# Scoring layer 1's heads once instead of twice in a two-layer cross-attention kernel, with the banks and stops around it rearranged

## The chip, the cores and the metric

The kernel runs on one core of one Trainium2 chip, as one launch. A core has five engines that run their own queues in order and wait for one another through semaphores: TensorE (PE: matrix products and transposes into the accumulators, PSUM), VectorE (DVE), ScalarE (ACT), GpSimd (POOL) and SyncE (SP, which here issues nearly all DMAs). PSUM has eight banks of 128 x 512 floats. The metric is the device time of the launch in microseconds, as the median of several runs. All data are 32-bit floats.

## The reference

Two cross-attention layers, one after the other, each with a residual. The batch is B = 4, queries S = 512, width C = 320, 20 heads of 16; the context has T = 1024 rows of E = 512.

```python
# layer 0: text = rows 0..1019 of the context, ip = its last 4 rows
q = heads(x @ W_q); k = heads(text @ W_k); v = heads(text @ W_v)
probs = softmax(q k^T / 4);  text_out = probs v
qsem  = l2norm(probs @ text_rows)            # every head times the whole context: the heavy product
fused = q k_ip^T / 4 + 0.5 * (qsem . l2norm(ip_rows))
ip_out = (softmax(fused) * mask) v_ip
x = (text_out + ip_out) @ W_out + b_out + x
# layer 1: text = rows 0..76, ip = rows 77..1023, each with its own softmax
q = heads(x @ Wq^T)
out = softmax(q k^T / 4) v  +  softmax(q k_ip^T / 4) v_ip
x = out @ Wo^T + bo + x
```

Layer 1 of a query tile needs layer 0 of the same tile, and nothing of other tiles.

## The kernel before

**Tiles.** Queries go in 16 tiles of 128 (`TURNS`, four per batch entry). The 20 heads go in groups of four, so that there are 80 groups of layer 0 (`G`). A group is two units (`Unit`) of two heads. A unit multiplies the exponentiated scores with the context by a scheme with seven block products in place of eight: each `product` is four fp32 products of 128 x 128 by 256 or 277 columns (the profile counts each as two matmuls, so x8). The seven lie in four parts: `part0` does "11" and "12"x"21", `part1` does "t1" and "s2"x"t2", `part2` does "12"x"22" and "21"x"t3", `part3` does "t4". The later ones add onto the banks of the earlier ones: "t4" is added onto the bank of "11" after DVE has read it in `part2` (`add_square(self.b1, ...)`, the second instruction named `c`).

**Scores of layer 0.** The next group's scores are made transposed (keys on partitions) by `fill`, in two halves. A head has only 16 channels, so four heads lie in four groups of 32 rows of the PE and are computed beside each other; such a stretch of matmuls is called a visit to the row groups here. ACT copies the scores to SBUF and DVE takes maxima of them. `max0` transposes the four heads' maxima (4 transposes), DVE reduces them and transposes the small result (`zt`), and since the maxima are needed along the free dimension of every partition they take a way through DRAM: four DMAs write `zd`, one DMA reads it back into all partitions (`bc`). `do_exp` then adds the negated maximum to the scores on DVE (`e<-e,bc`), and ACT exponentiates. The four additions of a group wait in the queue `ew`.

**Scores of layer 1.** They are computed twice. `do_max` computes them with the queries on partitions (name `mx`, 512 columns at a time), DVE reduces them to maxima; `do_sub` transposes these (`pt_nm`) and adds them as extra channels to the queries (`qa`); `do_exp` computes the scores again, transposed and with the maximum already subtracted (name `ex`), so that ACT can exponentiate straight from PSUM. `step(g, k)` does one quarter of a group: `mx` of the next group in two of the row groups and `ex` of this one in the other two. `do_pv` multiplies with the values (72 small matmuls); `normalise` divides by the sums.

**Order.** All is written out by hand: PE and DVE instructions are kept in program order, ACT, POOL and SP are ordered by a scheduler that respects dependences. After each part of a unit comes a stop, so a group has stops 0 to 7 (`stop(gi, k)`). Before, a stop takes one waiting item (a piece of layer 0's end, `late`, or of the next batch entry's projections, `proj`), then `fill0` at stops 0 and 1, a layer 1 quarter at stops 2, 4, 5 and 6, `max0` at stop 2, and additions from `ew` at stops 4 (one), 5 (two) and 6 (one). That makes six visits to the row groups per group. SP has among its DMAs the windows (`window`): after each of the products "11", "21", "t1" and "t4" a small DMA brings the next unit's value columns, and must wait on SP until PE has done with the old ones.

**PSUM.** Two double banks for scores (`ps_sc`), three banks for products (`qs0` to `qs2`, the unit's b1, b2, b3 in turn), one for everything else (`tp`).

## Time and profile before

| What | Value |
|---|---|
| Time, median of 3 runs (lowest, highest) | 3527.53 us (3527.39, 3540.56) |
| Profiled execution | 3535.14 us, of which the span is 3533.4 us |
| Mean granted TensorE clock | 0.981 of full speed |
| Busy: PE, DVE, ACT, POOL | 98%, 58%, 42%, 28% of the span |
| First product of a unit, end of the last one | 92.3 us and 3393.4 us into the span |
| DMA | 252.5 MB, 71 GB/s |

Busy time of an engine is the time in which at least one of its instructions is open. On PE, matmuls in different row groups and successive matmuls overlap, so the busy times of two groups of matmuls that run side by side must not be added. How long a stretch really holds the PE is read in the timeline, from the start of its first matmul to the start of what follows.

### The profile page before, as it was taken

Reading aid. Unit: us, or ns where it says so; the run is one execution under the profiler, and the core shown is the slowest. Engines: PE = TensorE matmul, PEld = TensorE weight load, DVE = VectorE, ACT = ScalarE, POOL = GpSimd, SP = SyncE. Lnnn points to the kernel's source line nnn. Section 1 sums busy time; section 2 is a strip of 40 time slices with the busy share of each in tenths; the row PEclk is TensorE's granted clock in tenths of the full one; section 3 lists DMA queues with packets and bytes.
Section 4 is the critical chain, followed back from the end, with each engine's and each line's share of the span. In section 5 each row is a group of like instructions: output and inputs, shape, how many; then the busy total and the mean of one; then the engine's idle time right before and its main releaser. Section 6 shows DMA issues by size and latency. Waiting matters only on the chain.

```text
span 3533.4 us, 74393 instructions
## 1 busy us (share of the span) xinstructions
PE 3446.9 (98%) x29092; PEld 2770.0 (78%) x29092; DVE 2066.4 (58%) x3894; ACT 1477.4 (42%) x2807; POOL 1004.2 (28%) x1066
## 2 busy tenths in 40 slices
PE   7999999999999999999999999999999999999989
PEld 6777777777788888887878888877877878788766
DVE  2444556666655655566665665666665666666644
ACT  1333344444434444444443443444444444454422
POOL 3322222332222222333222222222322322332310
PEclk9999999999999999999999999999999999999976
DMA  7454332222344234222234434222232222222211
GB/s 213 105 134 116 89 70 41 47 39 48 88 98 102 62 101 105 51 56 42 47 88 111 101 75 100 67 55 49 45 85 46 47 40 51 44 45 43 46 30 34
DMA packets 618013, 252.54 MB, mean 71 GB/s; under 512 B 484112, under 2 KB 591344, under 8 KB 617664
## 3 DMA queue, kind: packets, MB, share of 16 engines
q1 hardware_dynamic: 616624, 244.18, 29.8%
q8 instruction: 231, 3.78, 0.5%
q0 software_dynamic: 864, 3.41, 0.4%
q14 instruction: 118, 0.97, 0.1%
q10 hardware_dynamic: 176, 0.20, 0.0%
HBM read 206.63 MB, written 40.33 MB: 70 GB/s over the span
## 4 chain that ended last, share of the span: by engine, by line
PE 84%; DVE 8%; DMA 3%; issue 2%; SPq 2%; ACT 1%; POOL 0%; DVEq 0%; POOLq 0%; ACTq 0%
PE b L77 51%; PE ex L77 6%; PE pv L77 5%; PE sc L77 4%; PE pt_v L77 4%; PE mx L77 4%; PE pt_k L77 4%; DVE m L87 2%; PE pt_y L77 2%; PE pt_q L77 2%; DVE e L87 2%; DMA bc<-zd 1%; PE mx L92 1%; DVE den L87 1%; DVE n L87 1%
## 5 line engine op out<-in xcount | busy, mean ns | idle before, releaser
L77 PE MATMUL b<-xv_t,e 128*128 128x277 f32 x2560 | 678.6, 407 | 16.1 <-DVE c L87 14.7
L77 PE MATMUL b<-xv,e 128*128 128x277 f32 x2560 | 627.0, 397 | 2.8 <-ACT e L785 2.8
L77 PEld LDWEIGHTS b<-xv,e 128*128 128x128 f32 x2560 | 480.2, 190 | 119.3 <-ACT e L785 3.3
L77 PEld LDWEIGHTS b<-xv_t,e 128*128 128x128 f32 x2560 | 462.0, 190 | 139.1 <-DVE c L87 19.6
L785 ACT ACTIVATE e<-e 128x1024 f32<-128x1024 f32 x320 | 338.2, 1057 | 385.0 <-DVE e L87 373.4
L874 POOL TENSOR_TENSOR e<-e,s 128x512 f32<-128x512 f32 x160 | 203.3, 1271 | 1010.1 <-PE b L77 983.0
L87 DVE TENSOR_REDUCE m<-sc 128x256 f32<-128x1024 f32 (+1 forms) x320 | 341.7, 1088 | 163.7 <-PE sc L77 156.0
L87 DVE TENSOR_REDUCE m<-mx 128x2 f32<-128x870 f32 (+3 forms) x345 | 366.6, 1066 | 88.5 <-PE ex L77 67.4
L585 ACT ACTIVATE e<-ex 128x1024 f32<-128x1024 f32 x320 | 325.2, 1017 | 187.3 <-PE ex L77 186.8
L87 DVE TENSOR_TENSOR e<-e,bc 128x1024 f32<-128x1024 f32 x320 | 354.1, 1107 | 73.3 <-DMA bc<-zd 73.3
L524 ACT COPY e<-sc 128x1024 f32<-128x1024 f32 x320 | 322.6, 1011 | 173.8 <-PE sc L77 135.1
L859 ACT ACTIVATE junk<-c 128x256 f32<-128x256 f32 x480 | 198.9, 414 | 460.0 <-DVE c L87 455.4
L77 PE MATMUL mx<-kq,qq 16*128 16x512 f32 x1280 | 375.7, 662 | 6.5 <-DMA qq<-q1d 3.8
L77 PE MATMUL ex<-qa,kq 19*128 19x128 f32 x5120 | 377.4, 288 | 4.0 <-DVE qa L87 3.1
L87 DVE TENSOR_TENSOR c<-b,p 128x256 f32<-128x256 f32 x320 | 133.5, 417 | 407.7 <-PE b L77 399.9
L855 POOL TENSOR_TENSOR s<-e,e 128x512 f32<-128x512 f32 x160 | 203.5, 1272 | 468.9 <-ACT e L785 299.7
L77 PEld LDWEIGHTS ex<-qa,kq 19*128 19x128 f32 x5120 | 319.2, 191 | 16.4 <-issue 5.8
L77 PE MATMUL b<-xs,e 128*128 128x256 f32 x1280 | 321.5, 394 | 5.0 <-DVE sums L87 2.8
L787 POOL TENSOR_TENSOR e<-e 128x512 f32<-128x512 f32 x160 | 209.0, 1306 | 388.6 <-ACT e L785 388.4
L77 PE MATMUL b<-xs_t,e 128*128 128x256 f32 x1280 | 304.1, 381 | 0.0
L77 PE MATMUL b<-xs_t,s 128*128 128x256 f32 x1280 | 302.3, 379 | 0.0
L77 PEld LDWEIGHTS b<-xs_t,s 128*128 128x128 f32 x1280 | 242.4, 189 | 39.7 <-ACT p L873 0.5
(192 smaller groups left out, 4185.0 us busy)
## 6 DMA issues: line engine op xcount, KB each, us to landing
kq<-kd SPq DMA_DIRECT2D x640, 64.0 KB
v1q<-v1d SPq DMA_DIRECT2D x80, 373.5 KB
bc<-zd SPq DMA_DIRECT2D x80, 256.0 KB
xv<-v0d SPq DMA_DIRECT2D x320, 42.0 KB
xv_t<-v0d SPq DMA_DIRECT2D x320, 42.0 KB
L_xattn_W_k<-in_L_xattn_W_k_dram SPq DMA_DIRECT2D x13, 640.0 KB
L_xattn_Wv_ip<-in_L_xattn_Wv_ip_dram SPq DMA_DIRECT2D x13, 640.0 KB
raw<-in_ctx_dram SPq DMA_DIRECT2D x32, 256.0 KB
```

The source lines that it names most:

```text
L77: tc.keep_in_program_order(nc.tensor.matmul(out, lhsT=lhsT, rhs=rhs, start=start, stop=stop, skip_group_check=on))
L87: return lambda *args, **kw: keep(getattr(self.engine, name)(*args, **kw))
L92: tc.keep_in_program_order(nc.tensor.transpose(out, in_, ident))
L524: nc.scalar.copy(e[i].rearrange("p h t s -> p (h t s)"), ps[i].rearrange("p h n -> p (h n)"))
L585: nc.scalar.activation(e.rearrange("p i j s -> p (i j s)"), ps.rearrange("p i n -> p (i n)"), AF.Exp)
L785: nc.scalar.activation(flat, flat, AF.Exp)
L787: nc.gpsimd.tensor_tensor(e[:, 1], e[:, 1], e[:, 0], ALU.subtract)
L855: nc.gpsimd.tensor_tensor(self.s2, self.e("21"), self.e("22"), ALU.add)
L859: nc.scalar.activation(junk, x, AF.Square, accum_out=self.w["ss"][:, self.h + r, k : k + 1])
L874: nc.gpsimd.tensor_tensor(self.e("11"), self.e("11"), self.s2, ALU.add)
```

## The change

For all query tiles but the last, layer 1's scores are computed once, in the manner of layer 0 (class `Once`): `fill` makes them transposed in two halves, ACT copies them to SBUF, DVE takes maxima. `maxima` transposes eight tiles (the first key tile of each head, which holds the 77 text rows, and the maxima of the rest), DVE makes four small reductions or minima and one small transpose, four DMAs write the result to DRAM, and three DMAs read it back into all partitions: text maxima for partitions 0 to 76, the others' for 77 to 127 and for the other tiles. `do_exp` adds them on DVE (six additions per group in two shapes) and exponentiates from SBUF on ACT. `mx`, `ex`, `pt_nm` and `qa` are left only in the last tile (`twice`).

The stops are regrouped. Layer 0's `fill0` goes to stops 0 and 2, layer 1's `fill` to stops 4 and 6: four visits per group. The four odd stops take the additions: layer 1's two and two at stops 1 and 3, layer 0's two and two at stops 5 and 7. Projections and the items behind go to odd stops too. `maxima` of layer 1 comes between the two products of unit 0's `part0`, `max0` between those of unit 1's. The values of layer 1 (`add_values`) come at stop 4.

The general PSUM pool `tp` gets two banks, and the products only two: b2 and b3 of a unit now share one. There are four instead of six buffers for layer 1's scores.

```diff
-    e1p = pool("e1p", 6)
+    e1p = pool("e1p", 4)
-    ps_tp = pool("ps_tp", 1, space=PSUM)
+    ps_tp = pool("ps_tp", 2, space=PSUM)
...
-            self.bank = [f"qs{(2 * gi + i + k) % 3}" for k in range(3)]
+            self.bank = [f"qs{(i + k) % 2}" for k in (0, 1, 1)]
...
-        def part0(self):
+        def part0(self, between):
             self.product(self.b1, "11", "11", True)
...
+            between()
             self.product(self.b2, "12", "21", True)
...
+    def spread(zt, rows, tag, name):
+        zd = dr.tile([rows, P], F32, tag=tag, name=f"{tag}{name}")
+        for k in range(P // ZW):
+            nc.sync.dma_start(zd[:, ZW * k : ZW * (k + 1)], zt[ZW * k : ZW * k + rows, :])
+        return zd
...
+    class Once:
+        def fill(self, c):
...
+            self.e[c] = fill(1, self.k, c, self.m, e1p, "e1", self.name)
...
+        def maxima(self):
+            first, rest = [tp(f"mx{self.name}_{k}").rearrange("p (h t) -> p h t", h=4) for k in range(2)]
+            for h in range(4):
+                tr(first[:, h, :], self.e[0][h // 2][:, h % 2, 0, :], ident)
+            for h in range(4):
+                tr(rest[:, h, :], self.m[:, 0, h, :], ident)
+            z = zz[1]
+            vec.tensor_reduce(z[:, 0:4], first[:, :, 0:NTXT1], AX.X, ALU.max, negate=True)
+            vec.tensor_reduce(z[:, 8:12], first[:, :, NTXT1:], AX.X, ALU.max, negate=True)
+            vec.tensor_reduce(z[:, 4:8], rest, AX.X, ALU.max, negate=True)
+            vec.tensor_tensor(z[:, 4:8], z[:, 4:8], z[:, 8:12], ALU.min)
+            zt = st2.tile([P, ZW], F32, tag="zt", name=f"zt{self.name}")
+            vec.transpose(zt, z)
+            zd = spread(zt, 8, "zd1", self.name)
+            self.bc = bc = big.tile([P, 2, 4, P], F32, tag="bc1", name=f"bc{self.name}")
+            keep(nc.sync.dma_start(bc[:NTXT1, 0], zd[0:4, :].partition_broadcast(NTXT1)))
+            keep(nc.sync.dma_start(bc[NTXT1:, 0], zd[4:8, :].partition_broadcast(P - NTXT1)))
+            keep(nc.sync.dma_start(bc[:, 1], zd[4:8, :].partition_broadcast(P)))
+            self.v = load_values(self.z, self.turn, self.g)
+
+        def do_exp(self, c, i):
+            e, (first, rest) = self.e[c][i], [self.bc[:, k, 2 * i : 2 * i + 2, :] for k in range(2)]
+            if c == 0:
+                vec.tensor_tensor(e[:, :, 0, :], e[:, :, 0, :], first, ALU.add)
+            x = e[:, :, 1 - c :, :]
+            vec.tensor_tensor(x, x, rest.unsqueeze(2).to_broadcast([P, 2, TH - 1 + c, P]), ALU.add)
+            flat = e.rearrange("p h t s -> p (h t s)")
+            nc.scalar.activation(flat, flat, AF.Exp)
...
+    def visit(gi, k):
+        if k < 4:
+            fill0(gi + 1, k // 2)
+        if k == 4:
+            do_values()
+            begin()
+            do_fill(0)
+        if k == 6:
+            do_fill(1)
+
     def stop(gi, k):
-        behind = k == 0 and after
-        if not behind:
-            item()
-        if k < 2:
-            fill0(gi + 1, k)
-        if behind:
-            after.popleft()()
-        if k in (2, 4, 5) or k == 6 and gi < len(G) - 2 or ending[0] and k < 2:
-            l1_step()
-        if k == 2:
-            max0(gi + 1)
-        end_stop(k)
+        if k in (1, 3):
+            do_adds(2)
+        elif k % 2:
+            for _ in range(2):
+                item(ew)
+        if k % 2:
+            item(after, late)
+            item(proj)
+        else:
+            if k:
+                item(late)
+            visit(gi, k)
+        if k == 3:
+            item(norm)
+        stops[0] += 1
...
-            for k, part in enumerate((u.part0, u.part1, u.part2, u.part3)):
+            between = (lambda: max0(gi + 1)) if i else do_maxima
+            for k, part in enumerate((lambda: u.part0(between), u.part1, u.part2, u.part3)):
                 part()
                 stop(gi, 4 * i + k)
```

The order of the built instructions shows what the scheduler makes of it on SP: between the four DMAs that write layer 1's maxima and the three that read them back stands the window of "21" in most groups, and the window of "t1" in 39 of 75.

## The prediction

> **What bounds the kernel now.** I read the engines' busy shares first, then the PE timeline of a late group without projections, then DVE's waits, then DVE and SP around one round trip of the maxima.
>
> ```profile
> PE 3446.9 (98%) x29092; PEld 2770.0 (78%) x29092; DVE 2066.4 (58%) x3894; ACT 1477.4 (42%) x2807; POOL 1004.2 (28%) x1066
> ```
>
> PE is the bound; DVE has slack. By groups, `mx` is busy for 375.7 us and `ex` for 377.4 us, 9.4 us per group. That is not what they cost: they run in different row groups at once. The timeline of one group:
>
> ```profile
> 3287.49 1.17 PE L77 MATMUL sc<-qq,kq 16*128 16x128 f32 x32
> 3288.60 2.14 PE L77 MATMUL b<-xv_t,e 128*128 128x277 f32 x8
> ...
> 3297.15 0.70 PE L77 MATMUL mx<-kq,qq 16*128 16x512 f32 x2
> 3297.16 0.71 PE L77 MATMUL ex<-qa,kq 19*128 19x128 f32 x8
> 3297.68 0.59 PE L77 MATMUL mx<-kq,qq 16*128 16x512 f32 x2
> 3297.71 0.61 PE L77 MATMUL ex<-qa,kq 19*128 19x128 f32 x8
> 3298.25 0.66 PE L92 MATMUL mx<-ident,m 128*128 128x128 f32 x4
> 3298.75 2.04 PE L77 MATMUL b<-xv_t,e 128*128 128x277 f32 x8
> ...
> 3325.94 1.17 PE L77 MATMUL sc<-qq,kq 16*128 16x128 f32 x32
> ```
>
> From start to next start a visit costs 1.10 us, layer 0's (3287.49 to 3288.60) as a layer 1 quarter (3297.15 to 3298.25); four transposes cost 0.50. The period is 38.45 us, 35.76 without the output projection in it (2.69). All 80 groups, from 92.3 to 3393.4 us, average 41.3 with projections.
>
> ```profile
> DVE e L87 <- DMA bc<-zd: 73.3, 43, 4.6
> PE b L77 <- DVE c L87: 14.7, 17, 1.6
> ...
> 2994.84 0.21 DVE L87 STREAM_TRANSPOSE zt<-zz 128x32 f32<-128x32 f32 x1
> 2995.26 1.28 SPq L772 DMA_DIRECT2D zd<-zt  x4
> 2998.59 0.34 SPq L774 DMA_DIRECT2D bc<-zd  x1
> 3002.16 1.23 DVE L87 TENSOR_TENSOR e<-e,bc 128x1024 f32<-128x1024 f32 x1 [0.64 <-DMA bc<-zd]
> ```
>
> The first two lines are us in total, times, longest. The others are the price of a round trip through DRAM: 7.1 us from the end of `zt` to the first addition (0.2 until SP issues, 3.3 from the first write's issue to the read's, 3.6 to the data). Even now, with nearly two stops between `zt` and the first addition, DVE is late in 43 groups; PE rarely notices (14.7 us in all).
>
> **The change, part by part.**
>
> *PE.* Layer 1 costs 4 x 1.10 + 0.11 (`pt_nm`) = 4.51 us per group; after, 2 x 1.10 + 8 transposes at 0.12 = 3.15. It saves 1.36 in each of 75 groups (the last tile's five keep two scorings): **-102 us**. A plain group's PE work becomes 34.4.
>
> *DVE.* Gone per group: reductions 2 x (1.222 + 1.052 + 0.311), 2 x 0.218 and `qa` 0.29 = 5.9. New, by the nearest forms: reductions from the accumulators 2 x (0.957 + 1.220), maximum 0.69, three small reductions 0.47 + 0.36 + 0.68 (by columns, between 0.311 at 154 and 0.684 at 512), 0.2, `zt` 0.21, additions 2 x (0.40 + 0.988 + 1.226) = 12.2. So 6.3 x 75 = 475 us more, 2066 to about 2540: under PE, but a plain group's DVE work (these, layer 0's, `c`, `p`, `den`) sums to 31.1 of 34.4 us.
>
> *ACT, POOL, SP.* ACT gains four copies of 1.011 and 0.04 on each of four exponentials: 4.2 x 75, to about 1795 us. POOL's operations stay. SP issues seven more DMAs per group, 0.35 each, and about 512 KB more are read; `bc`'s three reads wait on SP behind the window of "21", in 39 of 75 groups behind that of "t1", and with them all later windows and loads.
>
> *The new wait.* DVE runs in order: the additions at stops 1 and 5 stand ahead of the two `c` of `part2`, and "t4" on PE waits for the second `c`. The maxima are now made only one part earlier. Plain group, us from the start of unit 0's "11":
>
> PE: "11" 1.9, eight transposes 2.9, "12"x"21" 4.8, visit 5.9, `part1` (3.80) 9.7, `part2` (3.65) 13.35, visit 14.45: ready for "t4".
> DVE: small reductions and `zt` 4.45; `c`, `pv`, reductions, `p` until 8.9; then idle. SP: write 4.5, reads from 7.8 (behind "t1"'s window 8.3) 0.35 apart, the last landing at 13.0 with 0.4 for twice the bytes. Additions until 15.3, two `c` 0.75: "t4" starts at 16.1, PE waits **1.7**.
> DVE goes on without a gap: reductions 1.9, 0.69, 0.96, `pv` 0.17, additions 2.45, `den` 2.19, `zz` and `zt` 0.9: 25.3. PE had its transposes at 20.5. "t1" of unit 1 writes the bank of `b2`, so it waits for `c` and `pv`: 25.85 against 25.6 (**0.25**, the cost of two banks). Maxima land at 25.3 + 7.1 = 32.4, additions 2.65, two `c`: 35.8; PE was ready at 34.4, waits **1.4**. The next "11" starts at 37.8, but DVE has reductions, maximum and additions (5.9) before layer 1's small reductions and comes to them 1.4 late, which returns at the next "t4" as 0.6 to 1. Period about **38.7**: DVE's 31.1 and two idle waits of some 4 us. The loop is DVE plus round trips, no more PE.
>
> *Groups without projections.* 45 steps for each of three batch entries and 13 at the start, four odd stops per group: 37 groups have projections, 43 none. The end of layer 0 and the output projection hold PE for 8.6 us per tile (the timeline's `pt_s` 0.3, `pt_p` 0.2, `pt_ip` 0.6, `pt_o` 0.4, `pt_y` 1.7, `pt_xT` 0.4, `pt_q` 2.2 and 2.7), DVE for some 9 by its rows: 1.6 to 1.7 of PE per group (five to a tile), and on DVE 1.8, of which I count 1.3, as the rest falls into its idle waits. After: 38.7 + 1.3 = 40.0, PE work 34.4 + 1.6 = 36.0, idle 4.0, against some 0.5 before: 43 x 3.5 = **+150 us**. Bounds: every wait hidden (-0.5 x 43 = -22), or both 2 us longer, as the longest wait for `bc` (4.6) against the average (1.7) shows to be possible (+320).
>
> *Groups with projections.* A step holds PE 1.0 to 3.6 us, and four of them cover the wait. Their evacuations (0.24 to 0.69) stand on DVE behind the additions: +1 in 32 groups with layer 1, **+32 us** (0 to +80).
>
> *Tail.* Before, 140 us lie behind the last product. After, one group of layer 1 and half another are left, and their waits for `bc` stand on DVE in front of layer 0's end: +8 to +16; with them finished early, the last tile runs alone from the queries' arrival (3429): -9. I take **+5** (-10 to +20). Six fewer to four buffers and the start cost nothing: the values at stop 4 free the scores before the next copy.
>
> Sum: -102 + 150 + 32 + 5 = +85 on the profiled execution's 3535.1: 3620. That execution stands 0.2% above the median, so **3612**.
>
> **Two rules against the rows.** A PE wait of 1.50 us in the tail, among sparse row-group matmuls, was followed by a lower clock:
>
> ```profile
> 3396.00:3398.60 2.60, 1.10 (x3) 0.29 (x2) 2.35 (x9) 0.89 (x2) 0.00 (x0) 1.00 0.10 25
> 3398.60:3402.40 3.80, 3.80 (x73) 3.35 (x72) 2.05 (x7) 0.00 (x0) 0.00 (x0) 0.56 0.02 4
> ```
>
> The last three columns are clock, DMA share and GB/s. Among dense products 1.25 us (3280.4 to 3281.7) did nothing: the mean clock from 3200 to 3350 is 1.00. My waits of 1.4 to 1.7 lie near both; I take no loss, and price the loss below. The Trainium skill (TensorE: Matmul & The Clock Gate, HAM oscillation) says that gaps above about 3.4 us lower the clock: by it the sum stays, since no wait here is so long; the tail's row speaks against it. The skill also gives about 2.0 us as fixed cost of a transfer (DMA: Bandwidth & Descriptors): two would make a round trip of some 4 us and the sum an estimated 3 us per round trip smaller, so faster than before; the row of 7.1 decides.
>
> **Rivals.**
> 1. *The waits are hidden; faster.* For it: PE's saving is sure, and before, DVE's 73 us of waiting cost PE 15. Against: the distance shrank to about 5 to 9 us of PE work. It decides where the 40.0 us fall below 38.0 (then 43 x 1.5 us of idle more than before, 32 and 5 use up the 102), that is with each round trip 1 us shorter than in my ledger. With no wait left at all: 3535 - 102 - 22 + 5 = 3416. With 36.8, little more idle than before: 3535 - 102 + 43 x 0.3 + 5 = 3451, by the median **3443**. Chance 0.20.
> 2. *About the same.* Half of the +150 and the rest as forecast: 3535 + 10, by the median **3537**. Chance 0.10.
> 3. *The clock falls after each wait.* One window of some 3.8 us at 0.56 loses 1.7 us, twice per plain group: 43 x 3.4 = 146 more, **3758**. Against it: dense products on both sides. Chance 0.07.
> 4. *Two banks cost.* If DVE is later still, "t1" waits for `c` and `pv` in both units, 1 us each in 75 groups: +150, **3762**. For it: the ledger gives DVE no gap before. Chance 0.05.
>
> **How the numbers follow.** The forecast has 0.58 and, by itself, 3560 to 3680. 0.5% (18 us) is about what a measurement can tell from no change. Faster by more: 0.20; within: 0.10; slower by more: 0.58 + 0.12 = 0.70. The range 3480 to 3720 leaves out some 0.10 below and 0.08 above.
>
> **What would show it.** Right: DVE's wait for `bc` grows from 73 to 400 us or more; PE's wait for `c` from 15 to some 200; PE busy falls to about 92%, DVE rises to about 70%; a plain group lasts 39 to 41 us with "t4" late twice. Wrong: a period near 36, or the read of `zd` landing before `p`. The weakest link is the round trip's length when SP has windows ahead of it.

## The result and the profile after

The changed kernel takes 4010.62 us (median of four, 4001.30 to 4016.56), beside 3533.48 us for the kernel before, measured in turn with it. The ratio is 1.1347, with a 95% interval from 1.1308 to 1.1386: 477 us slower. The forecast was 3612 us, with 3480 to 3720 as its range. The direction was right, the size was not.

From the page of the changed kernel: the span, the busy lines of PE and DVE, the granted clock in 40 slices, and the shares of the chain that ended last.

```profile
span 3999.4 us, 74611 instructions
...
PE 3484.2 (87%) x28417; PEld 2774.1 (69%) x28417; DVE 2656.5 (66%) x4413; ACT 1764.7 (44%) x3107; POOL 1063.3 (27%) x1066
...
PEclk9999999999999999999899999989999999999976
...
PE 47%; DVE 26%; DMA 12%; issue 6%; ACT 4%; SPq 3%; POOL 1%; DVEq 0%; POOLq 0%; ACTq 0%
```

PE is idle for 3999.4 - 3484.2 = 515 us, against 3533.4 - 3446.9 = 86 before: 429 us more. PE's busy time rose by 37 us as well, although a group's visits to the row groups went from six to four. Idle and busy together are the 466 us between the two spans. PE has 84% of the chain before, and 47% after.

The waits of PE (first five lines) and two of DVE's (last two lines) in the changed kernel: total us, times, longest.

```profile
PE b L77 <- DVE c L87: 132.6, 86, 4.5
PE b L77 <- DVE pv L87: 102.5, 38, 6.0
PE b L77 <- DMA zd<-zt: 33.9, 6, 6.7
PE mx L92 <- DVE zz L87: 33.6, 7, 4.9
PE mx L92 <- DVE xT L87: 29.8, 8, 4.6
...
DVE e L87 <- DMA bc<-zd: 497.3, 154, 7.0
...
DVE m L87 <- ACT e L519: 109.5, 144, 1.9
```

The first line is the wait that the forecast had: "t4" waits for the second `c`, which stands behind additions that wait for `bc`. The second is another one: "t1" waits for `c` and `pv` of `b2`, because `b2` lies in the bank that "t1" is to write. The third has the same place: it comes at the end of a tile, where the norms stand on DVE ahead of `c` and `pv`.

The name that the profile gives to a wait is that of the semaphore that moved last, and can be the wrong one. So the idle times in the brackets of PE's timeline were also added up by place in the group. "t1" of unit 0 is late by 150.5 us in all (41 times), "t1" of unit 1 by 23.5 (35 times), "t4" by 95.0 in unit 0 (47) and 37.6 in unit 1 (39), and the transposes ahead of "12"x"21" by 72.5 in unit 0 (17) and 24.1 in unit 1 (34). That is 403 of the 515 us. All 54 starts of "t1" that are over 0.3 us late come 0.2 to 0.35 us after the end of `pv`, whatever name the profile gives. The transposes of unit 0 (the fourth and fifth line are most of them) need a general bank: in 10 of the 17 places they start 0.06 us after DVE has copied a transposed input (`xT` or `cT`) out of one. These copies come behind the additions of stop 7. The last line is a wait of DVE itself: its second reduction of a visit reads the half of the scores that ACT copies first, and waits for that copy.

From the page's groups of the changed kernel, busy us and mean ns of one:

```profile
L77 PE MATMUL b<-xv_t,e 128*128 128x277 f32 x2560 | 785.0, 455 | 307.8 <-DVE c L87 132.6
```

Two groups of the changed kernel with different forms kept apart:

```profile
L87 DVE TENSOR_TENSOR e<-e,bc 128x1024 f32<-128x1024 f32 x310 | 431.4, 1412 | 195.2 <-DMA bc<-zd 195.2
...
L87 DVE TENSOR_TENSOR zz<-zz 128x4 f32<-128x4 f32 x75 | 42.5, 566 | 2.6
```

The same matmuls of "t1" and "t4" (the first group) were busy for 678.6 us before. The five groups of block products (tile `b`) together went from 678.6 + 627.0 + 321.5 + 304.1 + 302.3 = 2233.5 us to 785.0 + 684.8 + 326.4 + 304.6 + 302.4 = 2403.2 us, so by 170 us, for the same work; without them PE's busy time fell by 132 us. Additions of 1024 columns grew from 1226 to 1412 ns, and the minimum of four columns (`zz`) takes 566 ns on average.

One group without projections shows all of it. The timeline of PE, DVE, POOL and SP in the changed kernel (start, duration, engine, line; in brackets the idle time before it and its releaser); the group's "11" is the first line:

```profile
3532.59 2.03 PE L77 MATMUL b<-xv,e 128*128 128x277 f32 x8
...
3535.35 2.04 PE L77 MATMUL b<-xv,e 128*128 128x277 f32 x8
3537.32 1.17 PE L77 MATMUL sc<-qq,kq 16*128 16x128 f32 x32
3541.70 4.03 PE L77 MATMUL b<-xv_t,e 128*128 128x277 f32 x8 [3.21 <-DVE pv L87]
3545.52 2.95 PE L77 MATMUL b<-xs_t,s 128*128 128x256 f32 x8
...
3554.25 3.82 PE L77 MATMUL b<-xv_t,e 128*128 128x277 f32 x8 [1.22 <-DVE c L87]
```

```profile
3534.11 0.69 DVE L87 TENSOR_TENSOR m<-m 128x512 f32<-128x512 f32 x1
3534.72 0.17 DVE L87 TENSOR_TENSOR pv<-b,p 128x21 f32<-128x21 f32 x1
3534.81 3.19 DVE L87 TENSOR_TENSOR e<-e,bc 128x1024 f32<-128x1024 f32 x2
3537.92 0.47 DVE L87 SCALAR_TENSOR_TENSOR e<-e,drop,bc 128x256 f32<-128x256 f32 x1
3538.31 1.34 DVE L87 TENSOR_REDUCE zz<-mx 128x4 f32<-128x308 f32 x3
3539.69 1.11 DVE L87 TENSOR_TENSOR zz<-zz 128x4 f32<-128x4 f32 x1
3540.84 0.21 DVE L87 STREAM_TRANSPOSE zt<-zz 128x32 f32<-128x32 f32 x1
3540.97 0.38 DVE L87 TENSOR_TENSOR c<-b,p 128x256 f32<-128x256 f32 x1
3541.27 0.17 DVE L87 TENSOR_TENSOR pv<-b,p 128x21 f32<-128x21 f32 x1
...
3551.03 2.50 DVE L87 TENSOR_TENSOR e<-e,bc 128x256 f32<-128x256 f32 x4 [4.75 <-DMA bc<-zd]
```

```profile
3539.53 1.25 POOL L940 TENSOR_TENSOR e<-e,s 128x512 f32<-128x512 f32 x1
```

```profile
3541.08 1.30 SPq L531 DMA_DIRECT2D zd<-zt  x4
...
3545.76 0.38 SPq L886 DMA_DIRECT2D xv_t<-v0d  x1
3546.32 0.32 SPq L584 DMA_DIRECT2D bc<-zd  x1
```

DVE works from 3534.11 to 3541.44 without a gap: the maximum, the two additions of stop 7, the small reductions, `zt`, and only then `c` and `pv`. `b2` was done at 3537.4, and PE's visit at 3538.5. So "t1" starts at 3541.70, 3.21 us late. Then it takes 4.03 us in place of 2.1. Its window on SP (L886) waits for its end and stands ahead of the reads of `bc`, which go out at 3546.32; with the 3.3 us of before between the issues of the first write and of the first read it would be 3544.4. The additions wait 4.75 us for them, and "t4" is late by another 1.22 us and slow as well. `zt` ends 8.46 us after the start of "11"; the forecast's ledger had 4.45, or 5.85 with the 1.4 us of lateness that it names.

### The profile page after: what moved, and what is told of

Same layout as the page of the kernel before. It is cut to its first block, busy times and chain, and to the rows that moved or that the text cites. A ratio compares the mean times of both kernels' runs of the same rounds, so it can differ in the third digit from the quotient of the medians.

```text
span 3999.4 us, 74611 instructions
## 1 busy us (share of the span) xinstructions
PE 3484.2 (87%) x28417; PEld 2774.1 (69%) x28417; DVE 2656.5 (66%) x4413; ACT 1764.7 (44%) x3107; POOL 1063.3 (27%) x1066
## 3 DMA queue, kind: packets, MB, share of 16 engines
q8 instruction: 227, 3.72, 0.4%
## 4 chain that ended last, share of the span: by engine, by line
PE 47%; DVE 26%; DMA 12%; issue 6%; ACT 4%; SPq 3%; POOL 1%; DVEq 0%; POOLq 0%; ACTq 0%
PE b L77 28%; DVE e L87 12%; DMA bc<-zd 10%; DVE m L87 7%; PE sc L77 4%; PE pt_k L77 3%; PE pv L77 3%; DVE zz L87 3%; PE pt_v L77 3%; PE pt_q L77 2%; ACT e L519 1%; ACT junk L922 1%; DVE den L87 1%; PE mx L92 1%; DMA zd<-zt 1%
## 5 line engine op out<-in xcount | busy, mean ns | idle before, releaser
L87 DVE TENSOR_TENSOR e<-e,bc 128x768 f32<-128x768 f32 (+2 forms) x770 | 785.8, 1066 | 498.8 <-DMA bc<-zd 497.3
L77 PE MATMUL b<-xv_t,e 128*128 128x277 f32 x2560 | 785.0, 455 | 307.8 <-DVE c L87 132.6
L87 DVE TENSOR_REDUCE m<-sc 128x256 f32<-128x1024 f32 (+1 forms) x620 | 667.0, 1088 | 300.1 <-PE sc L77 186.1
L77 PE MATMUL b<-xv,e 128*128 128x277 f32 x2560 | 684.8, 412 | 2.8 <-ACT e L848 2.8
L519 ACT COPY e<-sc 128x1024 f32<-128x1024 f32 x620 | 610.4, 1007 | 103.9 <-PE sc L77 63.3
L937 POOL TENSOR_TENSOR e<-e,s 128x512 f32<-128x512 f32 x160 | 234.1, 1463 | 1297.1 <-PE b L77 1260.5
L596 ACT ACTIVATE e<-e 128x1024 f32<-128x1024 f32 x300 | 316.3, 1057 | 407.8 <-DVE e L87 394.7
L848 ACT ACTIVATE e<-e 128x1024 f32<-128x1024 f32 x320 | 337.7, 1057 | 340.2 <-DVE e L87 339.1
L77 PEld LDWEIGHTS sc<-qq,kq 16*128 16x128 f32 x9920 | 309.4, 188 | 106.6 <-issue 91.8
L77 PE MATMUL sc<-qq,kq 16*128 16x128 f32 x9920 | 369.1, 285 | 5.5 <-DVE m L87 3.3
L77 PE MATMUL b<-xs_t,s 128*128 128x256 f32 x1280 | 326.4, 401 | 0.0
L77 PE MATMUL b<-xs,e 128*128 128x256 f32 x1280 | 304.6, 381 | 0.0
L77 PE MATMUL b<-xs_t,e 128*128 128x256 f32 x1280 | 302.4, 379 | 0.0
L77 PEld LDWEIGHTS b<-xs_t,e 128*128 128x128 f32 x1280 | 243.2, 190 | 33.1
L77 PEld LDWEIGHTS b<-xs,e 128*128 128x128 f32 x1280 | 239.2, 190 | 36.3 <-issue 2.0
L940 POOL TENSOR_TENSOR e<-e,s 128x512 f32<-128x512 f32 x160 | 214.5, 1341 | 127.0 <-PE b L77 126.5
L77 PE MATMUL pv<-e,v1q 128*32 128x128 f32 x5760 | 195.2, 287 | 44.8 <-ACT e L596 27.4
```

The lines of the kernel that those rows point to most:

```text
L77: tc.keep_in_program_order(nc.tensor.matmul(out, lhsT=lhsT, rhs=rhs, start=start, stop=stop, skip_group_check=on))
L87: return lambda *args, **kw: keep(getattr(self.engine, name)(*args, **kw))
L519: nc.scalar.copy(e[i].rearrange("p h t s -> p (h t s)"), ps[i].rearrange("p h n -> p (h n)"))
L596: nc.scalar.activation(flat, flat, AF.Exp)
L848: nc.scalar.activation(flat, flat, AF.Exp)
L937: nc.gpsimd.tensor_tensor(self.e("11"), self.e("11"), self.s2, ALU.add)
```

## The experiments

Two theories at the start. A, the forecast's: the additions' wait for the maxima's round trip, ahead of the copies `c`, is the cost. B: the bank that "t1" shares is the larger one, through `c` and `pv` behind late DVE work and the clock after that wait. All edits are to the changed kernel unless another is named. The medians of the kernel before that stand beside the runs lie between 3530.9 and 3538.8 us, so the base moves by some 0.2% from run to run; executions of one version differ by up to 0.7% (e12).

**Three product banks (e1).**

```diff
-    ps_tp = pool("ps_tp", 2, space=PSUM)
+    ps_tp = pool("ps_tp", 1, space=PSUM)
...
-            self.bank = [f"qs{(i + k) % 2}" for k in (0, 1, 1)]
+            self.bank = [f"qs{(2 * gi + i + k) % 3}" for k in range(3)]
```

So that one general bank is enough, `maxima` now makes its first two reductions ahead of the second four transposes.

> Three product banks again, everything else as in the changed kernel (4010.6 us). Theory A, the forecast's: the additions' wait for the maxima's round trip, ahead of the copies c, is what the change costs. It would leave VectorE's wait for bc near 500 us and TensorE's wait for c near 130 us, and give 3960 to 4000 us. Theory B: the product bank that t1 shares is the larger cost, because t1 waits for copies that stand behind late VectorE work (102.5 us for pv), the clock falls after that wait (170 us more on the product rows), and the window of t1 holds the reads of bc back on SP. It would take the wait for pv to under 20 us, bring the product rows back from 2403 to about 2250 us, and give 3700 to 3800 us.

4284.76 us (ratio to before 1.2115, 1.2065 to 1.2166): both theories missed. PE's waits in it:

```profile
PE mx L92 <- DVE zz L87: 220.2, 75, 6.2
PE pv L77 <- DVE zz L87: 111.6, 38, 6.5
...
PE b L77 <- DVE c L87: 28.3, 18, 5.9
```

The wait of "t1" for `pv` is out of the list, and the one for `c` is down to 28.3 us. But now the one bank left for everything else is held by the first four transposes until DVE has reduced them, so the next four (`mx`), and layer 1's values (`pv`) behind layer 0's maxima, wait for the same late DVE. Eight banks aren't enough for both; the queue on DVE is the same, only which of PE's steps waits for it has changed. That speaks for the queue as the cause, and against the bank by itself.

**Additions behind both copies (e2).**

```diff
-        if k in (1, 3):
+        if k in (2, 3):
             do_adds(2)
-        elif k % 2:
+        elif k in (6, 7):
```

> The eight additions go to stops 2, 3, 6 and 7 in place of 1, 3, 5 and 7, so that none stands ahead of both copies c; banks as in the changed kernel. Theory A: TensorE's wait for c falls from 132.6 to under 40 us, VectorE's wait for bc from 497 to under 250 us, and the time to about 3750 us. Theory B: the wait of t1 for pv (102.5 us) and the low clock after it stay; the time falls by no more than 100 us, to 3900 us or more.

4133.25 us (1.1687, 1.1646 to 1.1728). DVE's wait for `bc` fell from 497 to 14.3 us, and the time rose by 123 us. What took its place on PE:

```profile
PE mx L92 <- DVE m L87: 184.2, 95, 2.6
PE b L77 <- DVE pv L87: 103.1, 47, 6.0
```

Two additions at stop 2 and two at stop 6 now stand ahead of a visit's reductions, the maximum and the transposes that need it. Theory A's 3750 fell. The wait for `pv` is untouched, as theory B had it.

**Additions that wait for nothing (e3).**

```diff
+    zc = cst.tile([P, 2, P], F32, name="zc")
...
+    nc.gpsimd.memset(zc, 0.0)
...
-            e, (first, rest) = self.e[c][i], [self.bc[:, k, 2 * i : 2 * i + 2, :] for k in range(2)]
+            e, (first, rest) = self.e[c][i], [zc, zc]
...
-            e, mine = es[gi, i, c], bc[:, 2 * i : 2 * i + 2, :]
+            e, mine = es[gi, i, c], zc
```

> The eight additions of a group read a constant tile of zeros instead of the maxima: maxima, transposes, DRAM writes and reads of bc are all still issued, but no addition waits for them. It leaves out the subtraction of the maximum from the scores. Theory A: all of VectorE's wait for bc (497 us) and TensorE's wait for c (132.6 us) go, and the time falls to 3550 to 3620 us. Theory B: t1 still waits for pv behind the second maxima's reductions, with the low clock after it: 3750 us or more.

3859.10 us (1.0912, 1.0873 to 1.0951): the wait for the round trips is worth 151 us here, and 323 us over the kernel before remain without it. PE's largest wait:

```profile
PE b L77 <- DVE pv L87: 116.5, 41, 5.6
```

The matmuls of "t1" and "t4" stay slow, 764.0 us in place of 785.0. Theory B's expectation held.

**Windows of "21" and "t1" behind "t4" (e4).**

```diff
+            self.put_off = []
...
-            if n in xv:
+            if n in ("21", "t1"):
+                self.put_off.append(n)
+            elif n in xv:
                 window(*self.next, n)
+            if n == "t4":
+                for n in self.put_off:
+                    window(*self.next, n)
```

> The two loads of value windows that SP issues behind the products 21 and t1 are put off until after t4, so that the reads of bc no longer stand behind them in SP's queue; nothing else moves. Theory A (the round trip is late by itself): no more than 20 us, 3990 us or more. Theory B (bc is held back by the window of t1, which waits for t1, which waits for its bank): in the half of the groups where it happens, bc lands 3 to 4 us earlier, and the time falls by 60 to 100 us, to 3910 to 3950 us; the wait of t1 for pv stays at about 100 us.

4137.93 us (1.1700, 1.1636 to 1.1765). The wait for `bc` fell from 497 to 223 us, but the windows themselves came too late:

```profile
PE b L77 <- DMA xv<-v0d: 265.9, 96, 6.5
```

The run doesn't tell what holding `bc` back on SP costs; the edit costs more than it can show.

**Two product banks in the kernel before (e5).**

```diff
-    ps_tp = pool("ps_tp", 1, space=PSUM)
+    ps_tp = pool("ps_tp", 2, space=PSUM)
...
-            self.bank = [f"qs{(2 * gi + i + k) % 3}" for k in range(3)]
+            self.bank = [f"qs{(i + k) % 2}" for k in (0, 1, 1)]
```

> The kernel before with the changed kernel's banks alone: two for the products, two for everything else; layer 1's scores still twice, additions where they were. Theory B (the bank that t1 shares costs by itself): t1 waits for c and pv in every unit, product rows slower, 3600 to 3700 us. Theory C (the bank costs only where VectorE's queue is long: here VectorE has 6.3 us less to do per group than in the changed kernel): 3530 to 3560 us, TensorE's wait for pv under 20 us.

3565.92 us beside 3536.89 (1.0080, 1.0056 to 1.0104): 29 us. PE's two largest waits:

```profile
PE b L77 <- DVE pv L87: 36.8, 48, 1.9
PE b L77 <- DVE c L87: 12.5, 17, 1.6
```

The wait for `pv` comes with the bank, 0.77 us each time. By the groups of PE 25.8 us of it stand ahead of "12"x"21", which now writes the bank of the last unit's `b1`, and only 11.0 ahead of "t1". DVE has some 8 us less to do per group here (2656.5 - 2071.2 us over 75 groups), which is a likely reason why it stays short; the run alone doesn't show it. The truth lies a little outside theory C's 3530 to 3560, and its wait for `pv` of under 20 us was missed too.

**Layer 1's additions left out (e6).**

```diff
-            if c == 0:
-                vec.tensor_tensor(e[:, :, 0, :], e[:, :, 0, :], first, ALU.add)
-            x = e[:, :, 1 - c :, :]
-            vec.tensor_tensor(x, x, rest.unsqueeze(2).to_broadcast([P, 2, TH - 1 + c, P]), ALU.add)
             flat = e.rearrange("p h t s -> p (h t s)")
```

> The changed kernel without layer 1's additions: the exponentials read the scores as they are, so the subtraction of the maximum is left out of layer 1 (its maxima, transposes and reads of bc are still made). VectorE loses 0.40 + 0.40 + 2 x 1.0 + 2 x 1.3, some 5.4 us per group or 400 us, and layer 0's additions still wait for their bc. Theory C (VectorE's queue is the cause): TensorE's wait for pv falls from 102.5 to under 30 us, the product rows from 2403 to under 2300 us, the time to 3480 to 3600 us. Theory B in the strict sense (the shared bank costs whatever the load): 3750 us or more. Theory A alone (the round trips): half of them are gone, 3850 to 3930 us.

3729.30 us (1.0542, 1.0511 to 1.0573): 281 us less, more than theory A alone had and less than theory C. PE's wait for `c` fell to 17.9 us, but that for `pv` is 122.6 us, in 39 places. The additions that were taken away are not those that hold `pv` up in unit 0; those are layer 0's at stop 7, and they are still there ("t1" of unit 0 is late by 167.9 us). DVE's busy time fell by 373 us, to 2283.5, so for this wait DVE's total load is not the measure; what counts is what stands ahead of `c` and `pv`.

**PE kept busy through the wait (e7).** The small products go into the bank of unit 0's first sums and change what these add up to; all else is the changed kernel's.

```diff
-            self.b1, self.b2 = self.psum(0)[:, 0:WIN], self.psum(1)[:, 0:WIN]
+            whole = self.psum(0)
+            self.b1, self.idle = whole[:, 0:WIN], whole[:, 384:512]
+            self.b2 = self.psum(1)[:, 0:WIN]
...
+            if self.i == 0:
+                for _ in range(24):
+                    mm(self.idle, ident, ident, True, True)
             self.b3 = self.psum(2)[:, 0:WIN]
             self.product(self.b3, "11", "t1", True)
```

> 24 small products of the identity with itself, into unused columns of unit 0's first bank, go onto TensorE ahead of t1 in unit 0, where the changed kernel's longest waits are. They add at least 24 x 0.11 us = 2.6 us in 80 groups, 211 us, to TensorE's work. If the clock's fall after a wait is a large part of the cost, the product rows come back from 2403 to 2330 us or less, and the time stays within 60 us of 4010. If the waits cost only their own length and the work does not fill them, the time rises by 100 to 210 us, to 4110 or more, and the product rows stay near 2400 us.

4106.75 us (1.1609, 1.1572 to 1.1646). Two groups of it:

```profile
L77 PE MATMUL b<-xv_t,e 128*128 128x277 f32 x2560 | 699.0, 416 | 83.5 <-DVE c L87 52.0
...
L77 PE MATMUL b<-ident 128*128 128x128 f32 x3840 | 449.9, 277 | 0.2 <-ACT p L938 0.2
```

The fill holds PE for 450 us, not the 211 that the expectation had, and the time rose by 96 us. The block products came back from 2403 to 699.0 + 679.8 + 304.6 + 304.1 + 302.4 = 2290 us, and the mean clock from 0.935 to 0.962; PE's idle time fell from 515 to 4111.1 - 3822.5 = 289 us. In that sum 450 - 113 - 226 = 111 us stand against the 112 us by which the span grew. So the rows came back as in the first case and the time rose nearly as in the second: the slow products are a consequence of the waits, worth some 110 us, and not of what the products read.

**Work on DVE moved behind `c` and `pv` (e9).** `first` is a new queue that holds a tile's norms.

```diff
+    first = deque()
...
-        norms()
+        first.append(norms) if turn + 1 < len(TURNS) else norms()
...
-            for _ in range(2):
+            for _ in range(2 if k == 5 else 1):
                 item(ew)
...
-        if k == 3:
+        if k == 0:
+            item(ew)
             item(norm)
+            item(first)
```

> VectorE's work that stands ahead of b2's c and pv is put behind them: den of layer 1 and the norms at a tile's end move from stop 3 and the end of the tile to stop 0, and layer 0's fourth addition from stop 7 to stop 0 of the next group, all behind the visit's reductions. Nothing is left out, banks and round trips stay. Theories B and C: TensorE's wait for pv falls from 102.5 to under 40 us, the 6.7 us waits at a tile's end go, product rows to about 2300 us, time 3780 to 3880 us. Theory A alone: 3980 us or more.

3726.04 us (1.0533, 1.0505 to 1.0561): 285 us less than the changed kernel, with all of its work, its banks and its round trips. This is more than the expectation had. PE's waits:

```profile
PE b L77 <- DVE p L87: 98.8, 46, 4.9
PE b L77 <- DVE c L87: 42.3, 27, 4.4
...
PE b L77 <- DVE pv L87: 13.0, 17, 3.1
```

The wait for `pv` is nearly gone; the moved work delays `p`, which follows it. By place, "t1" of unit 0 is late by 12.4 us in place of 150.5, and the transposes of unit 0 by 16.3 in place of 72.5, as one addition fewer stands ahead of the general banks' copies too. So the 285 us are not those of one bank alone. Theory A alone (3980 or more) is out.

**The same, where DVE waits for `bc` anyway (e10).**

```diff
+        first.append(norms) if turn + 1 < len(TURNS) else norms()
...
+        if k == 1:
+            item(first)
+            item(ew)
+        if k == 5:
+            item(norm)
         if k in (1, 3):
             do_adds(2)
         elif k % 2:
-            for _ in range(2):
+            for _ in range(2 if k == 5 else 1):
...
-        if k == 3:
-            item(norm)
```

> As the run with norms and an addition moved, but the moved work goes where VectorE waits for bc anyway: the norms of a tile's end and layer 0's fourth addition to stop 1, den to stop 5, each ahead of the additions there and behind p. Nothing is left out. In the run before this one, work at stop 0 delayed p and TensorE waited 98.8 us for it. If VectorE's queue ahead of c, pv and p is the cause, that wait falls under 25 us, the wait for pv stays under 20, and the time is 3560 to 3640 us. If the queue is simply too long wherever the work stands, the waits come back as waits for c (42 to over 120 us) and the time stays at 3700 us or more.

3712.78 us (1.0502, 1.0481 to 1.0524), not clear of e9's interval: the second case. `p` is out of the list, `c` is back at 128.4 us, `pv` has 54.3. In this order DVE has hardly a place where two us of work delay nothing.

**`b2` taken out of its bank by ACT (e11), and both (e12).**

```diff
...
-            self.add_square(self.b2[:, 0:EH], self.p1[:, 0:EH], 0, 0)
-            vec.tensor_tensor(self.values(0), self.b2[:, EH:], self.p1[:, EH:], ALU.add)
+            p2 = big.tile([P, WIN], F32, tag="p2", name=f"p2_{self.name}")
+            nc.scalar.copy(p2, self.b2)
+            self.add_square(p2[:, 0:EH], self.p1[:, 0:EH], 0, 0)
+            vec.tensor_tensor(self.values(0), p2[:, EH:], self.p1[:, EH:], ALU.add)
```

> The changed kernel with one difference: ScalarE copies b2 to SBUF as soon as the product is done, and VectorE makes c and pv from that copy, so that the bank t1 writes comes free without VectorE. (To make room for the copy, the squares' unused outputs go over their inputs or over u.) VectorE's order and its waits for bc are unchanged. If the shared bank behind VectorE's queue is the cause: the wait for pv (102.5 us) goes, what comes in its place is a wait for ScalarE's copy of under 40 us, the product rows fall from 2403 to 2300 us, and the time to 3700 to 3800 us. ScalarE is in order too and its exponentials wait for additions, so some of it stays. Theory A alone (round trips): 3980 us or more.

> Both at once: the order of the run e10 and ScalarE's copy of b2. If the bank and VectorE's order are the same cause, the two gains don't add up: 3550 to 3630 us, within 30 us of e10. If they are separate costs they add up, to 3500 us or less, under the kernel before. The wait for the round trips (c) stays in all cases: TensorE's wait for c 40 to 100 us.

e11: 3922.87 us (1.1088, 1.1060 to 1.1116), 88 us less than the changed kernel, less than half of the expected gain. The wait for `pv` is gone from the list, and PE waits for `c` for 159.5 us. But "t1" of unit 0 is still late, by 80.6 us in 34 places. The profile names POOL for most of them; yet every one starts 0.10 us after ACT's copy of `b2`. ACT too is in order, and in the group below the copy stands behind an exponential that waits for a late addition on DVE:

```profile
3288.21 1.06 ACT L848 ACTIVATE e<-e 128x1024 f32<-128x1024 f32 x1 [2.30 <-DVE e L87]
3289.17 0.38 ACT L941 COPY p<-b 128x277 f32<-128x277 f32 x1
3289.64 2.11 PE L77 MATMUL b<-xv_t,e 128*128 128x277 f32 x8 [2.24 <-POOL e L939]
```

So e11 didn't free the bank early, and its 88 us don't price the bank.

e12: 3665.55 us (1.0358, 1.0331 to 1.0385), 47 us less than e10. "t1" of unit 0 no longer waits at all. The copy's 88 us shrank to 47 beside e10's order: neither case came out cleanly, as the time is 36 us over the expected range of the first, 47 us from e10 where 30 were allowed, and far from the 3500 of the second. The wait for `c`, 136.8 us, is over its expected 40 to 100. Its waits, and two starts of "t4" in one stretch of it:

```profile
PE b L77 <- DVE c L87: 136.8, 88, 5.2
...
PE b L77 <- DVE p L87: 17.5, 23, 0.8
```

```profile
3262.28 3.72 PE L77 MATMUL b<-xv_t,e 128*128 128x277 f32 x8 [1.89 <-DVE c L87]
...
3301.22 2.14 PE L77 MATMUL b<-xv_t,e 128*128 128x277 f32 x8 [1.89 <-DVE c L87]
```

One group is 3301.22 - 3262.28 = 38.94 us long, and "t4" of unit 0 is 1.89 us late. The forecast's ledger had 38.7 and 1.7. With the bank and DVE's order out of the way, this kernel comes nearest to the one that the ledger describes. Its other parts differ: in this stretch "t4" of unit 1 is 0.20 us late (1.4 in the ledger), `p` holds PE up for 0.82 (nothing there), and the first "t4" takes 1.58 us more than the second (no loss there).

**What is left of e12 (e13, e15, e16).** e13 takes layer 1's additions behind both copies without putting them ahead of the reductions; e15 is e13 without ACT's copy.

```diff
+        if k == 2:
+            do_adds(1)
         if k == 4:
-            do_values()
-            begin()
-            do_fill(0)
+            do_adds(2)
...
-        if k in (1, 3):
-            do_adds(2)
+        if k == 1:
+            item(first)
+            item(norm)
+            item(ew)
+        if k == 3:
+            do_adds(1)
+        if k == 5:
+            do_values()
+            begin()
+            do_fill(0)
```

> ScalarE's copy of b2 as in e12, and layer 1's additions one at stop 2 behind the visit's reductions, one at stop 3 and two at stop 4, its values and the first half of its next scores at stop 5; den and layer 0's fourth addition to stop 1. So no addition waits for bc ahead of a copy c, and every round trip has about two more parts of PE work to hide in. If what is left of e12 (127 us over the kernel before, TensorE's wait for c 136.8 us) is the round trips, as the forecast's ledger has it, the wait for c falls under 40 us and the time to 3480 to 3560 us. If it is VectorE's sheer work per group (31 us and more of 35), the waits move to p, mx or pv and the time stays at 3620 us or more.

> As e13 without ScalarE's copy of b2: only the order of stops differs from the changed kernel, nothing is left out. If the shared bank costs once VectorE's queue ahead of it is short: 30 to 60 us more than e13 (29 us is what two banks cost in the kernel before). If not, within 15 us of e13.

e13: 3721.32 us (1.0549, 1.0527 to 1.0572), e15: 3760.09 us (1.0643, 1.0622 to 1.0664). The wait for `bc` is 47.7 us in e13, and the time is 56 us longer than in e12. PE's waits in e13:

```profile
PE b L77 <- DVE c L87: 62.1, 55, 5.0
PE b L77 <- DVE pv L87: 53.8, 41, 1.9
```

There the waits moved, as the second case had it. ACT's copy is worth 39 us at this point, as e15's first case had it. Since e13 moves several things at once, e16 takes from e12 nothing but the wait:

> As e12, with the additions reading a constant tile of zeros in place of the maxima (the subtraction of the maximum is left out; all else is issued). If the round trips are what is left of e12: TensorE's wait for c falls from 136.8 to under 30 us and the time to 3500 to 3550 us. If VectorE's work per group is: 3620 us or more, with the waits for c at 80 us or more though nothing waits for bc.

The edit is that of e3, in e12. 3559.82 us (1.0068, 1.0051 to 1.0085), 106 us less than e12:

```profile
PE b L77 <- DVE c L87: 48.5, 76, 2.3
```

The time is 10 us over the first case's range, and the wait for `c` 48.5 us where it had under 30; the second case is out. So the round trips are most of what is left in e12, 106 of 127 us over the kernel before. DVE's busy time is 2731.0 us in e16, more than the 2656.5 of the changed kernel, and the time 451 us less: DVE's sheer work isn't what the change costs. Of the rest, 25 us by e16's own comparison, no run tells the parts. PE is busy for 3341.3 us, 106 less than before, which is the forecast's saving, and idle for 218 in place of 86. e13 was no test of the round trips, since its new order made other waits.

**GpSimd beside VectorE (e14, e17).**

```diff
-            nc.gpsimd.tensor_tensor(self.e("11"), self.e("11"), self.s2, ALU.add)
...
-            nc.gpsimd.tensor_tensor(self.e("12"), self.e("12"), self.s2, ALU.subtract)
```

> The changed kernel without GpSimd's two operations per unit on the exponentials, e11 plus s2 and e12 minus s2 (left out; the sums that t1 and the second half of the block products take are then others). If GpSimd's work beside VectorE's lengthens VectorE's queue enough to matter, layer 1's and layer 0's additions of 1024 elements fall from 1.41 to about 1.23 us, the small minimum of the maxima from 0.57 to 0.2 us, and the time by 80 to 200 us, to 3810 to 3930. If not, under 40 us, 3970 or more.

> As e12, without GpSimd's two operations per unit on the exponentials (e11 plus s2, e12 minus s2; left out, so the products that read them are others). If VectorE's work, lengthened beside GpSimd, is what is left of e12: the wait for c falls under 80 us and the time to 3560 to 3620 us. If the round trips are: the wait for c stays above 110 us, 3640 us or more.

e14, in the changed kernel: 3829.50 us (1.0842, 1.0808 to 1.0876), 181 us less. Additions of 1024 columns take 1244 ns in it, in place of 1412; the small minimum is at 621, in place of 566, and not near the 0.2 us expected, as it now runs beside POOL operations that are left in (`s2` in 40 of 75 cases). e17, in e12: 3637.05 us (1.0279, 1.0257 to 1.0302), 28 us less, and the wait for `c` is 150.0 us, as for the round trips. What POOL's work costs thus depends on whether DVE is late ahead of the bank already. "t1" also needs `e11`, which POOL makes in the changed kernel; but that isn't what e14 took away there, since in the changed kernel every late "t1" follows `pv`. In e14 it still does: "t1" of unit 0 is late by 78.4 us in 33 places (the profile has them under `issue`), each 0.10 us after `pv`.

| Kernel | us | Ratio to before, 95% interval | PE's wait for c, pv, p (us) | DVE's wait for bc (us) | Clock |
|---|---|---|---|---|---|
| before | 3533.5 | 1 | 14.7, none, 1.0 | 73.3 | 0.981 |
| changed | 4010.6 | 1.1347 (1.1308 to 1.1386) | 132.6, 102.5, none | 497.3 | 0.935 |
| e3, no wait for bc | 3859.1 | 1.0912 (1.0873 to 1.0951) | 4.5, 116.5, none | 0 | 0.934 |
| e7, fill | 4106.8 | 1.1609 (1.1572 to 1.1646) | 52.0, 4.4, none | 287.0 | 0.962 |
| e9, order | 3726.0 | 1.0533 (1.0505 to 1.0561) | 42.3, 13.0, 98.8 | 262.5 | 0.963 |
| e10, order | 3712.8 | 1.0502 (1.0481 to 1.0524) | 128.4, 54.3, none | 266.7 | 0.963 |
| e12, order and copy | 3665.6 | 1.0358 (1.0331 to 1.0385) | 136.8, none, 17.5 | 193.7 | 0.958 |
| e16, e12 and no wait for bc | 3559.8 | 1.0068 (1.0051 to 1.0085) | 48.5, none, 16.7 | 0 | 0.979 |

The waits are by the profile's names. By place, "t1" of unit 0 is late by 150.5 us in the changed kernel, 161.2 in e3, 5.8 in e7 (behind the fill), 12.4 in e9, 57.9 in e10, and not at all in e12 and e16. None of these versions is faster than the kernel before.

## Why the prediction was right, and where it was wrong

**Right: the direction and its mechanism.** DVE's wait for `bc` was to grow to 400 us or more (497.3), and "t4" to wait for `c` behind it (132.6 us against some 200 forecast). Shown by e16 and e3: taking only the wait for `bc` away gains 106 us in e12 and 151 us in the changed kernel. The forecast's two sums for it were 150 + 32. The plain group of 38.7 us was met by e12, with 38.94, but in part by luck, as its parts differ. Where e12 stands 127 us over the kernel before, the forecast had 79.

**Right: PE's saving, ACT and the tail.** PE's busy time without the block products fell by 132 us (102 forecast, from path lengths and not busy times, so the two are near but not the same thing). ACT came to 1764.7 us (1795), the tail grew from 140 to 148 us (+5 forecast).

**Wrong: the step on the shared bank, "0.25, the cost of two banks".** That was one sentence in the ledger: "t1" of unit 1 finds `pv` ready at 25.85 against 25.6. For unit 1 it was about right: 75 x 0.25 us is 19, and "t1" of unit 1 is late by 23.5 in all. For unit 0 the ledger had no wait. There "t1" is late by 150.5 us, 3.2 us most often and 6.7 at the longest, each time just behind `pv`. The same late DVE empties the general banks, and the 72.5 us of the transposes ahead of "12"x"21" aren't in the ledger either. Moving DVE's work out of the way of both took 285 to 298 us off (e9, e10), the copy by ACT another 47 (e12); how much of that is the bank of "t1" alone, no run shows. Why the ledger missed it, by its own lines:
- *It took the queue for on time.* It let unit 0 begin with DVE's small reductions ending at 4.45 and then mentioned that DVE comes to them 1.4 us late. It charged that to the next "t4" alone. Everything that stands behind them, `c` and `pv` of `b2` first of all, is late too. In the trace the small reductions begin 5.72 us after "11", and `pv` ends 8.85 us after it, where PE is ready at 5.9.
- *It put DVE's two reductions of a visit back to back.* Between them DVE waits for ACT's copy: 1.16 us in the group shown (3531.69 to 3532.85), 109.5 us in 144 places (at most 7.7 us before).
- *It priced DVE's work by rows from a kernel in which an addition of 1024 columns rarely ran beside POOL (5 of 160; 118 of 310 in the changed kernel).* These additions were 1.226 us and took 1.412; the small minimum was 0.2 and took 0.57; DVE's busy time was to be 2540 us and is 2656.5.
- *It left out the end of a tile.* The norms, some 4 us on DVE, stood on DVE before as well, where PE's longest wait for `c` was 1.6 us; the ledger counted them as work, not as work ahead of a bank. In the first group of a tile "t1" of unit 0 is late by 68.2 us in all, in 14 places, and 33.9 of it stands under `zd`.

**Wrong: rivals 3 and 4 as alternatives.** Rival 4 named this wait (1 us in both units, 150 us, chance 0.05), rival 3 the falling clock (146 us, 0.07). The sum took no loss of clock; the block products lost 170 us. But neither is an alternative to the forecast. A late DVE holds the bank, the wait at the bank slows the products, and the late end of "t1" holds the reads of `bc` back on SP. Added up, 3612 + 150 + 146 = 3908, they come much nearer to 4010 than any one of them; the rest was in no rival.

**Wrong signs to look for.** PE busy was to be 92% and is 87%; a plain group was to last 39 to 41 us, and here it is 3576.98 - 3532.59 = 44.4. "t4" was to be late twice in it; in all groups it is late by 95.0 us in unit 0 and only 37.6 in unit 1.

**Open.** The parts don't sum: each edit shortens the same queue, so its worth depends on the others (181 and 28 us for POOL's two operations). How much the windows on SP cost by holding `bc` back wasn't settled (e4), nor were the last 25 us of e16; two shared banks took 29 us in e5, which is of that size, but that was another kernel.

## What to carry to other kernels

When an in-order engine is loaded more, list not only its sum but, for each accumulator bank it empties, everything that stands ahead of the emptying instruction, at the durations it has beside other engines; a bank saved is a place where a late engine stops PE. When several rivals are consequences of one lateness, add them and don't choose among them. And if such a wait has to go, first reorder the late engine's queue: here that gave 285 us with nothing left out, while one more bank, taken from the transposes, cost 274. Where the profile's name for a wait seems odd, see which instruction of those that must come first ends at a fixed distance ahead of every late start.

## What the runs showed of the hardware

- *A late PE is also a slow PE, after waits shorter than expected.* In the group shown, a wait of 3.21 us was followed by a product of 4.03 us in place of 2.1; in e12, two waits of 1.89 us at the same place, one group apart, were followed by 3.72 and 2.14 us. The granted clock over these three products was 0.50, 0.55 and 1.00. From 1500 to 3300 us of the changed kernel, 65 of 529 products of eight matmuls took over 2.4 us, 81 us more than 2.1 us each. The Trainium skill (TensorE: Matmul & The Clock Gate, HAM oscillation — how this bites in real kernels) names gaps above about 3.4 us. Here shorter ones were enough, and the same length did and didn't do it.
- *Two SBUF operands on DVE wait for POOL.* The minimum of 4 columns at 3539.69 took 1.11 us and ended 0.02 us after POOL's operation that was open from 3539.53 to 3540.78; all 27 of its fellows with no POOL operation beside them take 0.16, and 47 of the 48 others end within 0.06 us of the end of one. Additions of 1024 columns take 1.22 us in 192 places without POOL and 1.72 in 118 beside it. The reductions of 1024 scores, which read accumulators, take 1.22 us either way. The Trainium skill (SBUF — State Buffer, Who interferes with whom) has this rule, that a VectorE instruction with two SBUF inputs and a GpSimd instruction that reads SBUF exclude each other. This trace agrees. The rule spoke against this change, which puts eight such additions per group on DVE where there were four, and the forecast didn't weigh it.
